# A decoder layer on one core: cross-attention scores from 12-bit halves in two halves of the array, feed-forward biases as matmul rows, Silu out of PSUM

## Chip, core and metric

One core of a Trainium2 chip runs the whole kernel in one launch. The metric is the device time in microseconds (us). A difference of about 0.3% (5.5 us) is what the measurement can tell from no change.

## What is computed

The reference is one post-norm decoder layer over 32 batches of 128 tokens, model width 512, all in float32:

```python
x = layernorm(x + attn(x, Wq, Wk, Wv, Wo))        # 16 heads of 32, rotary, causal
x = layernorm(x + xattn(x, ctx, ctx, gamma))      # 8 heads over the token axis
x = layernorm(x + ffn(x, w1, b1, ln_g, ln_b, w2, b2))

def xattn(q, k, v, gamma):     # q, k, v: [32, 128, 512], read as [batch, 8 heads, 16, 512]
    qk = einsum('bhdq,bhdl->bhql', qh, kh) / 4    # contracts 16 tokens: 512 x 512 per head
    return gamma * einsum('bhql,bhdl->bhdq', softmax(qk), vh)

def ffn(x):
    h = silu(bitlinear158(x, w1, b1))             # 512 -> 2048
    h = gelu(h)                                   # exact
    h = layer_norm(h, ln_g, ln_b)
    return bitlinear158(h, w2, b2)                # 2048 -> 512

def bitlinear158(x, w, b):     # rows of rms-normalized x to int8 steps, w to {-1, 0, 1}
    return act_quant(rms_norm(x)) @ weight_quant(w).T + b
```

## The kernel before

**Two phases.** The first phase does the self attention of all 32 batches and leaves in DRAM, for each batch, the normalized result (`x1d`), the parts of the cross attention's queries (`qd`) and keys (`kd`), and the values beside columns of ones (`cd`). The second phase does cross attention and feed-forward, batch by batch.

**The order of the work** is found by a planner (`Plan`) while the program is built. Every step is put in with `pl.op(kind, cost, fn, ins, outs, prio)`. `run` takes, again and again, the step that could start first by the given costs; ties within `slack` go by `prio` plus an offset of its kind (`OFF1`, `OFF2`). Steps of one kind keep their order. The instructions of each engine (PE, DVE, ACT, POOL, SP) are then held in the order found. Tiles come from rings: a new tile of a tag waits until the one n before it has been read. `rel` keeps a transfer from being planned before a time; in the second phase this is 30 us a batch. SP issues every DMA.

**First phase, for each batch**: `stage_q` projects queries, keys and values from float32 numbers held in two 12-bit parts (float32r), three products of parts each (`project`, L322). `stage_s` computes scores on 32 rows of the array (L419), masks them, takes the softmax, and transposes (L442). `stage_o` weighs the values (L461), applies Wo, adds x and normalizes. `split3` (L326 to L340) cuts the result and the context into three bfloat16 parts: two casts to bfloat16 (L330 on DVE, L335 on ACT), two subtractions (L333 on POOL, L336 on DVE), and six stores each (L339), because the six rows of parts of a token lie side by side in DRAM. `early` loads the operands of the first batches when the last projection has been put in. The feed-forward weights are cut to {-1, 0, 1} on the way.

**Second phase, for each batch:**

- `load` fetches operands of four heads at a time: `kp` and `qp`, 96 rows (6 rows of parts for each of 16 tokens), one DMA each (L626).
- `b1_` finds the largest score of each query: 32 matmuls of 96 rows by 512 columns (`mx`, L653), each reduced by DVE (L657). `shift` cuts its negative into three bfloat16 parts by five small operations (on POOL, L676 to L680; on DVE for the last five batches, L670 to L673), transposes them (L685, L687) and stores them as rows 96 to 98 of `qp` (L691).
- `b2_` computes the scores again, transposed, with the three rows more: 32 matmuls (`sT`, L746), each followed by an Exp out of PSUM (L749 on ACT). For each 128 keys, four heads are weighed and summed side by side, each in 32 columns of the array, in float32 (`acc`, L756). The ones beside the values give the sums of the weights.
- `final` stores the sums (L767), loads them turned (L828, L829), divides (L832, L833, L839), adds x1 and normalizes.
- `up_` scales the rows to int8 steps (`scales`, L854 to L866; `steps`, L880 and L883), adds b2 to a copy of x2 (L920), turns the steps by a DMA transpose (L922) and multiplies with w1 in four pieces of 512 columns (L933), in one bank of PSUM. DVE takes each piece out: z = piece x scale + b1 (L936).
- `gelu_` does Silu and Gelu over 2048 columns in SBUF (L948, L950). ACT loads a function table ahead of Silu, of Gelu and of the next Exp.
- `down_` takes the layer norm over 2048 columns (sums of squares on ACT, L963; one quarter normalized on ACT, L780, three on POOL, L784; ln_g and ln_b on POOL, L980; in the last five batches on DVE, L988 and L999), the mean square (L1005) and the largest value (L1006), the steps (`q2`: half on ACT, L897, half on DVE, L899, as int16, then a cast on DVE, L902), the transpose (L1011), 16 matmuls with w2 (L1017), the sum with x2 + b2 (L1021), the last norm and the store (L1024).

PSUM's banks in the second phase: three `mx`, three `sT`, one `acc`, one `m` for both feed-forward products.

Of the kernel before, what the change touches and what calls it, by code (L numbers as in the profile page):

```python
# [11 lines left out]
F32 = mybir.dt.float32  # L12
# [12 lines left out]
NB = 32  # batches  # L25
S = 128  # tokens of a batch
D = 512  # model width
NH = 16  # heads of the self attention
HD = D // NH
XH = 8  # heads of the cross attention, over the token axis  # L30
XD = S // XH
DI = 2048  # width of the feed-forward part
# [3 lines left out]
MAGIC = 12582912.0  # 1.5 * 2**23: adding it rounds to the nearest even integer  # L36
NEG = -1e30

# A float32 number is the sum of three bfloat16 parts a, b, c.  The scores of the cross attention
# contract 16 tokens only, so the products of the parts lie side by side on the contraction axis:  # L40
# six rows of parts for each token, and three rows that take the parts of the shift away.
Q_PARTS = (0, 1, 2, 0, 1, 0)
K_PARTS = (0, 0, 0, 1, 1, 2)
NPR = 6 * XD
NROW = NPR + 3

# columns of the constants
# [4 lines left out]
def constants():  # L52
    """Rotary tables by position."""
# [10 lines left out]
CFG = dict(y0e='Pool', x2be='Pool', q2T=1, q1=2, tb2=5, boost=1.0, bank_mT='mx', bank_q1T='m', bank_z='m', bank_q2T='mx', bank_py='m', early=5, gm=1, ssv=1, NQ=4, cT=3, f=2, num=1, x1=2, rden=2, x2=2, nb=32, mx=3, sT=3, acc=1, m=1, ex=8, mTe='DVE', acce='ACT', q1e='ACT', q2e='ACT', mse='Pool', lne='Pool', ye='Pool', sce='Pool', mxw=1, stw=1, pair=1, z=3, xb=3, slack=0.126, last_mse='DVE', last_lne='DVE', last_ye='Pool', last_sce='DVE', last_y0e='Pool', last_bank_mT='sT', last_bank_q1T='m', last_bank_z='m', last_bank_q2T='mx', last_bank_py='sT', zm='APPP', last_zm='F', q1m='mp', q2m='ad', last_q1m='mp', last_q2m='d')  # L64
OFF2 = {'Pool.zt': 32.97, 'Pool.zb': 10.12, 'SP.q1T': -33.89, 'SP.q2T': -25.03, 'SP.const': 8.3, 'x.kq': 7.58, 'SP.v': 6.3, 'PE.mx': 32.55, 'DVE.mx': 46.29, 'Pool.ms': -11.15, 'PE.mT': -51.04, 'DVE.mT': -18.04, 'SP.m': -65.66, 'PE.sT': -34.55, 'ACT.ex': -64.48, 'PE.pv': 35.35, 'ACT.acc': -108.33, 'SP.f': 28.74, 'SP.fd': 34.31, 'SP.fn': -21.32, 'SP.fx': -30.95, 'DVE.rd': -5.27, 'SP.fr': -64.53, 'SP.fb': -9.3, 'Pool.y': -5.46, 'DVE.y': -83.63, 'DVE.c1': 49.52, 'Pool.c1': -87.98, 'Pool.x2b': 9.33, 'PE.c1': 38.82, 'DVE.z': -130.28, 'ACT.gelu': 43.8, 'DVE.nmu': -9.46, 'ACT.sq': 102.74, 'Pool.zn': 16.77, 'ACT.sq2': 71.51, 'DVE.am2': 94.88, 'Pool.c2': -54.15, 'DVE.q2': -34.78, 'PE.c2': 62.57, 'DVE.c3': 95.97, 'Pool.c3': -68.79, 'SP.out': -62.35, 'SP.kq': 54.02, 'DVE.zn': 19.87, 'DVE.q2a': -3.2, 'DVE.ms': 82.72, 'DVE.zb': 34.45, 'ACT.q2a': 7.79, 'Pool.q1a': -75.82, 'DVE.q1': 41.56, 'Pool.yn': 0.05, 'Pool.c1m': 7.06, 'ACT.zt': -9.94, 'Pool.c2m': -14.95, 'Pool.c3n': 10.85, 'DVE.yn': 22.22, 'DVE.c1m': 4.44, 'DVE.c2m': -7.16, 'DVE.c3n': 10.04}
# [3 lines left out]
class Buf:  # L69
    """A tile that its first write allocates; n tiles of its tag rotate."""  # L70

    def __init__(self, tag, make):
        self.tag, self.make, self.t = tag, make, None
        self.left, self.free_at = 0, 0.0
        self.readers, self.writers = [], []


class Op:
    __slots__ = ("kind", "engine", "cost", "fn", "deps", "bufs", "new", "at", "rel", "prio", "end", "lat")


class Plan:
# [57 lines left out]
    def start(self, o):  # L140
# [5 lines left out]
        for b in o.new:  # L146
            n, hist = self.tags[b.tag][:2]
            if len(hist) >= n:
                if hist[-n].left:
                    return None  # L150
# [942 lines left out]
```

## Time and profile before

| | us |
|---|---|
| three executions | 1843.21, 1847.17, 1843.22 |
| median | 1843.22 |
| span of the profiled execution, first to last instruction | 1837.6 |
| median less span | 5.6 |
| busy: PE, DVE, ACT, POOL | 1694.8, 1630.8, 1337.6, 1256.5 |

The span is that of one profiled execution; the profile holds no other time of it. The first phase's last matmul starts near 681 us, the second phase's first near 683 us.

How to read its rows. A group row has the line of the kernel, the engine, the operation, the tiles (out<-in), their shapes and the count; after the bar the busy time of the group, the mean in ns of one instruction, then the engine's idle time just ahead of them and what ended it. A row of the chain of waits has a start, a length and what the end hung on in that time. In the slices each digit is the busy tenth of a fortieth of the span. PE's busy time is modelled from pipelined matmuls: a full row doesn't mean peak speed.

### The profile page before, as it was taken

What the parts mean: (1) busy time and instruction counts of PE and PEld (TensorE: products, weight loads), DVE (VectorE), ACT (ScalarE), POOL (GpSimd) and SP (SyncE); (2) the same over time, 40 slices, a digit from 0 to 9 for tenths busy, and PEclk for the clock granted to TensorE, in tenths of its full rate; (3) what the DMA queues carried; (4) which work ended last, traced back from release to release, by engine and by line L of the source; (5) the groups of instructions that cost most, each with busy time, mean ns of one, the idle gap of its engine ahead of it and who ended that gap; (6) DMA issues with size and microseconds to landing.
All of it is one profiled execution on the core that took longest, in us unless ns stands there. A gap on an engine that the chain in (4) does not pass through costs nothing.

```text
span 1837.6 us, 29788 instructions
## 1 busy us (share of the span) xinstructions
PE 1694.8 (92%) x9540; PEld 848.8 (46%) x9540; DVE 1630.8 (89%) x2811; ACT 1337.6 (73%) x2811; POOL 1256.5 (68%) x1903
## 2 busy tenths in 40 slices
PE   6999999999999989999999999999999998889864
PEld 5877777777777762232323333333333322222221
DVE  7789998889988868898989999999999989999885
ACT  3556545664545544789999989999999979878862
POOL 4466666656656550467798989899889986775562
PEclk9999999999999987998999999999999999989976
DMA  6466656665654564543545455454544543533422
GB/s 197 136 212 210 193 191 205 210 212 187 203 175 161 174 212 171 149 116 106 148 122 159 110 134 147 126 149 117 151 137 128 154 118 110 147 106 102 97 61 57
DMA packets 237733, 275.75 MB, mean 150 GB/s; under 512 B 112124, under 2 KB 161276, under 8 KB 237192
## 3 DMA queue, kind: packets, MB, share of 16 engines
q1 hardware_dynamic: 237576, 273.85, 50.2%
q8 instruction: 75, 1.23, 0.3%
q14 instruction: 82, 0.67, 0.1%
HBM read 150.82 MB, written 101.20 MB: 137 GB/s over the span
## 4 chain that ended last, share of the span: by engine, by line
PE 47%; DVE 23%; DMA 9%; ACT 7%; POOL 6%; issue 4%; SPq 1%; DVEq 0%; POOLq 0%; ACTq 0%
PE mm L322 14%; DVE mt L657 7%; PE sT L746 7%; PE acc L756 7%; PE mx L653 6%; PE sc L419 5%; ACT ex L749 3%; PE m L933 3%; PE m L1017 2%; DMA qd<-sp 2%; PE tr L442 2%; DMA q2T<-q 1%; DVE z L936 1%; DVE pr L422 1%; DMA qp<-qd 1%
## 5 line engine op out<-in xcount | busy, mean ns | idle before, releaser
L657 DVE TENSOR_REDUCE mt<-mx 128x1 f32<-128x512 f32 x1024 | 642.4, 678 | 42.7 <-PE mx L653 41.5
L749 ACT ACTIVATE ex<-sT 128x512 f32<-128x512 f32 x1024 | 535.6, 618 | 90.7 <-PE sT L746 71.8
L653 PE MATMUL mx<-kp,qp 96*128 96x512 bf16 x1024 | 342.3, 393 | 34.4 <-DVE mt L657 28.4
L746 PE MATMUL sT<-qp,kp 99*128 99x512 bf16 x1024 | 322.9, 388 | 10.8 <-ACT ex L749 6.3
L756 PE MATMUL acc<-ex,cT 128*32 128x512 f32 x2048 | 275.7, 613 | 0.7 <-DMA cT<-cd 0.7
L430 ACT ACTIVATE pr<-pr,nm 128x128 f32<-128x128 f32 x512 | 199.5, 392 | 103.9 <-DVE nm L425 87.2
L653 PEld LDWEIGHTS <-qp 96*128 96x128 bf16 x1024 | 96.5, 99 | 221.9 <-issue 120.9
L746 PEld LDWEIGHTS <-kp 99*128 99x128 bf16 x1024 | 88.3, 98 | 222.5 <-issue 146.5
L445 ACT COPY prT<-tr 128x512 f32<-128x512 f32 x96 | 52.9, 587 | 149.2 <-PE tr L442 149.0
L419 PE MATMUL sc<-qkT,qkT 32*128 32x128 f32 x1024 | 147.8, 283 | 11.6 <-DVE pr L422 11.1
L933 PE MATMUL m<-w1q,q1T 128*128 128x512 fp8e4 x512 | 137.4, 392 | 22.0 <-DVE z L936 12.4
L419 PEld LDWEIGHTS sc<-qkT,qkT 32*128 32x128 f32 x1024 | 123.4, 186 | 52.2 <-DVE pr L422 22.1
L980 POOL TENSOR_TENSOR z<-z,g_b 128x512 f32<-128x512 f32 x108 | 139.5, 1302 | 4.9 <-ACT z L780 4.3
L980 POOL TENSOR_TENSOR z<-z,bb_b 128x512 f32<-128x512 f32 x108 | 139.8, 1301 | 1.4
L435 POOL TENSOR_TENSOR pr<-pr,rd 128x512 f32<-128x512 f32 x96 | 106.4, 1108 | 45.9 <-DVE rd L433 31.8
L386 POOL TENSOR_TENSOR ra<-ra,rb 128x256 f32<-128x256 f32 x64 | 47.3, 738 | 117.4 <-DVE rb L381 117.1
L1017 PE MATMUL m<-w2q,q2T 128*128 128x512 fp8e4 x432 | 112.3, 388 | 3.8 <-DMA q2T<-q 2.8
L422 DVE TENSOR_TENSOR pr<-sc,cmask 128x512 f32<-128x512 f32 x128 | 86.8, 678 | 18.3 <-PE sc L419 10.1
L1017 PEld LDWEIGHTS <-q2T 128*128 128x128 f16 x512 | 52.3, 104 | 105.0 <-DMA q2T<-q 29.1
L936 DVE SCALAR_TENSOR_TENSOR z<-m,dq,b_b 128x512 f32<-128x512 f32 x128 | 94.9, 741 | 6.0 <-PE m L933 5.4
L430 ACT ACTIVATION_READ_ACCUMULATOR pr<-pr,nm 128x1 f32 x512 | 96.5, 189 | 0.0
L756 PEld LDWEIGHTS acc<-ex,cT 128*32 128x32 f32 x2048 | 41.2, 108 | 119.5 <-issue 112.8
(159 smaller groups left out, 3475.3 us busy)
## 6 DMA issues: line engine op xcount, KB each, us to landing
kd<-sp SPq DMA_DIRECT2D x192, 128.0 KB
qd<-sp SPq DMA_DIRECT2D x192, 128.0 KB
kp<-kd SPq DMA_DIRECT2D x64, 384.0 KB
qp<-qd SPq DMA_DIRECT2D x64, 384.0 KB
cd<-v SPq DMA_DIRECT2D x32, 512.0 KB
cT<-cd SPq DMA_DIRECT2D x32, 512.0 KB
F<-f SPq DMA_DIRECT2D x64, 256.0 KB
xt<-in_xT SPq DMA_DIRECT2D x32, 256.0 KB
```

The source lines that it names most:

```text
L322: nc.tensor.matmul(pq.t, parts[a].t[:, c, :], w[t][:, c, sl], start=k == 0, stop=k == 11)
L419: nc.tensor.matmul(sc.t[:, c * P:(c + 1) * P], qT.t[r, c, :], kT.t[r, c, :], start=True, stop=True)
L430: nc.scalar.activation(pr.t[:, c, :], pr.t[:, c, :], AF.Exp, bias=nm.t[:, c:c + 1], accum_out=den.t[:, c:c + 1])
L653: nc.tensor.matmul(sc.t[:, j, :], q.t[0:NPR, h, (qc + j) * P:(qc + j + 1) * P], k.t[0:NPR, h, :], start=True, stop=True)
L657: pl.op("DVE.mx", 0.064 + 0.534 * W, lambda: nc.vector.tensor_reduce(mt.t[:, i:i + W], sc.t, AX.X, ALU.max), (sc,), (mt,), p, join=True)
L746: nc.tensor.matmul(sc.t[:, i, :], k.t[:, h, lc * P:(lc + 1) * P], q.t[:, h, :], start=True, stop=True)
L749: pl.op("ACT.ex", 0.052 + 0.426 * SW, lambda: nc.scalar.activation(ex.t[:, j:j + SW, :], sc.t, AF.Exp, scale=1.0 / XD ** 0.5), (sc,), (ex, ...
L756: nc.tensor.matmul(acc.t[32 * h:32 * h + 32, :], v.t[:, XH * lc + 4 * g + h, :], exs[h // 2].t[:, h % 2, :], start=lc == 0, stop=lc == NC - 1)
L933: nc.tensor.matmul(flat(pz)[:, i * 512:(i + 1) * 512], q1T.t[:, c, :], w1q[:, c, (n + i) * 512:(n + i + 1) * 512], start=c == 0, stop=c == ...
L936: pl.op("DVE.z", 0.13 + 0.535 * W, lambda: nc.vector.scalar_tensor_tensor(z.t[:, sl], flat(pz), dq1.t, b1_b[:, sl], ALU.mult, ALU.add), (p ...
L980: pl.op(e + kind, 0.148 + 0.0021 * w if e == "Pool" else 0.05 + 0.00105 * w, lambda: en(e).tensor_tensor(t(), t(), other[:, sl], op), src, ...
L1017: nc.tensor.matmul(flat(py)[:, 0:D], q2T.t[:, c, :], w2q[:, c, :], start=c == 0, stop=c == NI - 1)
```

## The change

1. **Two 12-bit parts for three bfloat16 parts.** `split3` becomes `split2`: a rounding to float32r (ACT) and one subtraction (POOL for the context, DVE for the queries), and two stores of twice the size in place of six. Scores are hi x hi + lo x hi + hi x lo: 48 rows for 16 tokens. The shift is one row, no longer three: `shift` has only a transpose and a negating copy on DVE; its five small operations go, and of three stores two are left.
2. **Two heads in halves of the array.** One head's 48 or 49 rows lie on partitions 0 to 48, the next one's on 64 to 112. Each matmul of `mx` and `sT` then names rows of one half, and the planner takes a matmul right behind one in the other half as costing 0.06 us. `fetch` needs four DMAs for a tile, where one did.
3. **Biases as matmul rows.** b1 and b2 are kept in two 12-bit parts as rows (`rows1`, `rows2`). For each quantization the inverse of the back scale is formed in parts on DVE, transposed on PE and copied by DVE to `uT`; a matmul of three rows adds bias / scale to the product in PSUM. The bias add on DVE (L936) and x2 + b2 on POOL (L920) go, and the copies of b1 and b2 on all partitions.
4. **Silu read from PSUM**, with the scale, four times 512 columns. From the first Silu of a batch to its Gelu the planner puts no Exp between ("window"), and counts 1.28 us for a change of table.
5. Placement: all quarters of the layer norm on POOL (`zm='PPPP'`), q2's steps on POOL with the rounding on DVE (`q2m='mp'`); any of eight PSUM banks for any use, `m=2`; more tiles of `x2`, `z`, `q1T`; the weighing of all but the first 128 keys planned in two halves of 256 columns; 29 us a batch in `rel`; new offsets.

```diff
-def split3(kind, v, dst, parts, prio): ...
+def split2(kind, v, dst, prio):
+    sp = pl.buf("sp")
+    e, e1 = C1[kind + '_hi'], C1[kind + '_lo']
     pl.op(f"{e}.{kind}", ..., lambda: cp(e)(sp.t[:, 0, :], v.t), (v,), (sp,), prio)
+    pl.op(f"{e1}.{kind}l", ..., lambda: en(e1).tensor_tensor(
+        sp.t[:, 1, :], v.t, sp.t[:, 0, :].bitcast(F32), ALU.subtract), (v, sp), (sp,), prio)
+    for s in range(2):
+        dma(kind, lambda s=s: nc.sync.dma_start(dst[s].rearrange("t h c -> h t c"), sp.t[:, s, :].bitcast(F32)), 262, ...)
...
+def fetch(t, d, g, keys):
+    rows = t.bitcast(F32).rearrange("(p r) j c -> p r j c", p=2)
+    src = d[:, :, 4 * g:4 * g + 4, :].rearrange("s t (p j) c -> p (s t) j c", p=2)
+    for p in range(2):
+        if keys:
+            nc.sync.dma_start(rows[p, 0:XD], src[p, 0:XD])
+            nc.sync.dma_start(rows[p, XD:NPR], src[p])
+        else:
+            nc.sync.dma_start(rows[p, 0:2 * XD], src[p])
+            nc.sync.dma_start(rows[p, 2 * XD:NPR], src[p, 0:XD])
...
+sc, i, r = pl.buf("mx"), 8 * h + 4 * j + qc, slice(HALF * h, HALF * h + NPR)
+pl.op("PE.mx", 0.23, lambda: nc.tensor.matmul(sc.t, q.t[r, j, qc * P:(qc + 1) * P], k.t[r, j, :],
+                                             start=True, stop=True), (q, k), (sc,), p, half=h)
...
+mT, pt = pl.buf("mT"), bank(b, 'mT')
+pl.op("PE.mT", 0.12, lambda: nc.tensor.transpose(flat(pt)[0:16, 0:P], mt.t, ident), (mt,), (pt,), at)
+pl.op("DVE.mT", 0.2, lambda: nc.vector.tensor_scalar(mT.t, flat(pt)[0:16, 0:P], -1.0, None, ALU.mult), (pt,), (mT,), at)
...
+def inverse():
+    e = en(e2)
+    r = ut.t.rearrange("p (g r) -> p g r", r=32)
+    nc.vector.reciprocal(u.t, dq.t)
+    e.tensor_scalar(r[:, :, 0:3:2].bitcast(F32R), u.t.unsqueeze(2).to_broadcast([P, 4, 2]), 1.0, None, ALU.mult)
+    e.tensor_tensor(r[:, :, 1], u.t.to_broadcast([P, 4]), r[:, :, 0], ALU.subtract)
+pl.op(f"PE.{p}u", 0.12, lambda: nc.tensor.transpose(pt.t[:, 0:P], ut.t, ident), (ut,), (pt,), prio)
+pl.op(f"DVE.{p}u", 0.2, lambda: nc.vector.tensor_copy(uT.t, pt.t[:, 0:P]), (pt,), (uT,), prio)
...
-    pl.op("DVE.z", ..., lambda: nc.vector.scalar_tensor_tensor(z.t[:, sl], flat(pz), dq1.t, b1_b[:, sl], ALU.mult, ALU.add), ...)
+    def mm(cs, last=False):
+        for c in cs:
+            nc.tensor.matmul(pz.t, q1T.t[:, c, :], w1q[:, c, sl], start=c == 0, stop=False)
+        if last:
+            nc.tensor.matmul(pz.t, uT.t[32 * n:32 * n + 3, :], rows1[32 * n:32 * n + 3, :], start=False, stop=True)
+    pl.op("ACT.silu", 0.478, lambda: nc.scalar.activation(z.t[:, sl], pz.t, AF.Silu, scale=dq1.t),
+          (pz, dq1), (z,), at, join=True, tab="silu", win=win)
```

## The prediction

> **What bounds the kernel now.** I read the page's slices first, to find the stages.
>
> ```profile
> PE   6999999999999989999999999999999998889864
> DVE  7789998889988868898989999999999989999885
> ACT  3556545664545544789999989999999979878862
> POOL 4466666656656550467798989899889986775562
> ```
>
> Each digit is 46 us. Up to about 660 us (self attention) only PE is full. From 790 to 1440 all four engines are nearly full; then comes a thinning tail. The windows view by stage says how nearly (its columns: stretch and length, busy us of PE, PE loads, DVE, ACT, POOL):
>
> ```profile
> 184.00:552.00 368.00, 357.93 (x2398) 284.95 (x2396) 327.02 (x613) 198.60 (x739) 236.85 (x278) 0.99 0.60 197
> 1120.00:1443.00 323.00, 309.81 (x1610) 102.10 (x1606) 311.69 (x509) 304.69 (x459) 289.77 (x490) 0.99 0.50 137
> 1443.00:1700.00 257.00, 232.65 (x1163) 71.81 (x1156) 238.36 (x404) 217.15 (x329) 190.01 (x295) 0.95 0.45 120
> ```
>
> The second row holds ten batches (Gelu to Gelu), 32.3 us each: DVE 31.2, PE 31.0, ACT 30.5, POOL 29.0 us per batch. No engine has two microseconds to spare, so relief of one of them is worth at most the distance to the next. The costliest groups there:
>
> ```profile
> L657 DVE TENSOR_REDUCE mt<-mx 128x1 f32<-128x512 f32 x317 | 198.8, 677 | 6.0 <-PE mx L653 5.8
> L936 DVE SCALAR_TENSOR_TENSOR z<-m,dq,b_b 128x512 f32<-128x512 f32 x40 | 29.7, 742 | 2.0 <-PE m L933 1.6
> ```
>
> Last, the chain of waits between the phases:
>
> ```profile
> 663.57 7.87 DMA qd<-sp
> ...
> 677.42 5.37 DMA qd<-sp
> 682.81 5.41 DMA qd<-sp
> 688.24 5.41 DMA qd<-sp
> 693.67 5.41 DMA qd<-sp
> ...
> 711.01 0.99 PE acc L756 x8
> 712.00 0.75 PE sT L746 x3
> ...
> 721.35 0.65 PE mx L653 x3
> ```
>
> For 36 us the end hangs on stores of query parts, six DMAs a batch at 0.574 us of SP each. The last three lines price a change of PE's tiling: three full-array matmuls take 0.65 us after their like (0.217 each), 0.75 after the column-tiled weighing. In the records of the trace going in costs 0.09 as well: about 0.1 us per change.
>
> **Part 1: PE, cross-attention scores.** Removed: 64 bf16 matmuls a batch of 96 or 99 rows at 0.217 = 13.9 us. Added: 64 of 48 or 49 rows in 12-bit (f32r) form, alternately in the upper and lower half of the array. From the order of the changed kernel I count 800 places where two neighbours lie in different halves and 448 matmuls alone, so 25 pairs and 14 singles a batch. A single costs 0.234 (the spacing of the f32r projections, L322). No row shows a pair in row halves: at best it costs one stream, 0.22, at worst two singles, 0.47. The nearest row is the weighing, whose four column groups do run side by side (eight matmuls of 0.43 in 0.99); I take 0.26. Sum 25 x 0.26 + 14 x 0.234 = 9.8 us.
>
> Against this stands a rule of the Trainium skill ("TensorEngine Tiling (Array Packing)", Key Properties): changing the tiling mode drains TensorE. The lines above agree for column tiling, 0.1 us a time. The order has 603 runs of equal tiling in the second phase before and 1647 after: half-array scores, whole-array feed-forward, column-tiled sums and three-row bias matmuls alternate. That is 18.8 and 51.5 changes a batch, 1.9 us and 5.2 us. Without the rule PE would drop to 27.4 us; with it:
> before 13.9 + weighing 6.8 (8 x 0.85 streaming) + feed-forward 6.9 (32 x 0.217) + transposes 0.3 + changes 1.9 = 29.8;
> after 9.8 + 6.8 + 6.9 + bias rows 1.2 (5 x 0.234) + float32 transposes 0.9 (four of 0.22) + changes 5.2 = 30.8.
> What the halves win, the changes of tiling take back.
>
> **Part 2: DVE.** Removed: the bias add out of PSUM, 4 x 0.742 = 2.97 us a batch, and the half-and-half rounding of q2 (L899 1.25 + L902 0.97 = 2.2). Added: one float32-to-float16 step over 2048 columns (L883 takes 0.41 us at least for 512, so about 1.4, and there loses 0.7 waiting: 2.1). Further, twice a batch, the inverse scale: a reciprocal (0.165, L433), two tiny operations, a copy from PSUM (0.21, L687). Like operations on DVE are those of the shift in the last batches, in the groups of the page's view by line:
>
> ```profile
> L671 DVE SCALAR_TENSOR_TENSOR mr<-mt,ms 128x16 f32<-128x16 f32 x10 | 8.4, 837 | 0.3
> L670 DVE TENSOR_SCALAR ms<-mt 128x16 bf16<-128x16 f32 x10 | 5.4, 537 | 0.1
> ```
>
> Their shortest take 0.174 and 0.154. "SBUF — State Buffer" of the Trainium skill (Who interferes with whom) says that DVE operations with two SBUF inputs or in a two-port mode, and GpSimd, exclude each other for a whole instruction. With the shortest times the set costs 0.66 us; with a full GpSimd instruction (L671's median, 1.19) for both, 2.75. I take the mean wait of the four shift operations, 0.4 each: 1.33 a set, 2.7 a batch. DVE after: 31.2 - 2.97 - 2.2 + 2.1 + 2.7 = 30.8 (29.5 to 33.6).
>
> **Part 3: ACT and POOL.** ACT loses its half of q2 (1.2) and a quarter of the normalization (0.83); Silu in four pieces from PSUM costs 4 x 0.52 (the spacing of Exp, same form) against 1.91, +0.2. Table loads stay three a batch (93 in both orders). But Silu now waits for matmuls between two table loads, and no Exp may go between. Two banks hold the pieces; the third piece's five matmuls (4 x 0.217 + 0.234 + two changes 0.2 = 1.3 us) start when Silu 1 frees a bank and end 0.8 after Silu 2, and the fourth again 0.8 late: 1.6 us. Queued behind are all Exps, and PE behind three full score banks. ACT: 30.5 - 2.0 + 0.2 + 1.6 = 30.3. POOL loses the shift parts (2 x 1.24), x2 + b2 (1.27) and nb (0.19), gains a normalization quarter (0.79) and q2's 2048 columns (2.1 to 2.75, from L880's 0.685 for 512; I take 2.3): 28.1.
>
> **Part 4: SP and transfers.** Per batch 12 loads are added at 0.37 to 0.43 (16 small ones for 4) and two shift stores (0.58) go: +3.7 us, queued before shift stores and sums; some 14 us of issues become 18 of 32, so nothing to 0.3 us. In the first phase 8 of 12 stores a batch go (4.6 us of SP), and 2.2 us of DVE; but PE is 97% busy there and waited only 8.8 us for DVE between 200 and 550: -3 us (0 to -12).
>
> **Sum.** Steady, 22 batches: the busiest engine goes 31.2 to 30.8, but three engines now lie within 0.5, and PE, ACT and DVE wait for each other inside the Silu window. I let the period's excess over the busiest grow from 1.1 to 1.8: +0.3 a batch, +7. Between the phases: the chain's five last batches need 1.5 us of SP each where they took 4.3 to 4.7, but the early operand loads grow from 12 to 40 DMAs (+10 us): -12 (-20 to +5). Filling (700 to 790, PE the chain): -5. Tail, where DVE is 93% busy: shift parts of ten groups 22.4 us gone (L670 to L673), bias adds 14.9, inverse scales +13.5: -24, of which the last 50 us, a chain of q2T transposes and matmuls at half clock, hide a quarter: -18. Total 7 - 12 - 5 - 18 - 3 = -31. The profiled span of 1837.6 would become 1807; the median of the runs is 5.6 above that span, so 1812.
>
> **Rivals.**
> - *Likeliest (0.42)*: as summed, 1812, its own range 1790 to 1850.
> - *The period falls (0.20)*: pairs at 0.22 (PE 29.8), tiny DVE operations rarely blocked (29.5), Silu's waits filled. The period loses 1.3 instead of gaining 0.3: 35 better, 1777. For it speaks that bank waits already hide some changes of tiling; against it, GpSimd at 90%.
> - *Slower, PE (0.14)*: the halves do not run side by side. 64 x 0.234 = 15.0 puts PE at 36.0 and the period above 36: +4 x 22 = +88, so about 1893. It decides from a pair time of 0.27 to 0.29, where PE passes DVE. For it: no row of before has row halves at work. Against: column groups do it.
> - *Slower, DVE (0.14)*: each tiny operation waits out a GpSimd instruction: DVE 33.6, +2.8 x 22 = +62, half of the tail's gain gone: near 1870. L671's median is for it; the other three shift operations are usually short.
> - *Nothing (0.10)*: losses and gains of the ends cancel within 0.3% (5.5 us, about what can be told from no change): 1843.
>
> Chances: of the first case 0.36 lie below 1837.7 and 0.06, where the tail's gain fails, above 1848.7. Faster 0.36 + 0.20 = 0.56; the same 0.10; slower 0.14 + 0.14 + 0.06 = 0.34. The range leaves out the PE case and the best of the second: 1768 to 1875.
>
> **What would show it.** In the changed profile: the score matmuls' spacing in pairs (0.26 or 0.47) and PE's chain pieces after each change of tiling; the mean of the two inverse-scale operations on DVE against 0.15; ACT's idle before Silu waiting for PE (1.6 us a batch); Gelu-to-Gelu 32.6; the first Exp of the second phase near 690 instead of 706. I am wrong if the steady period moves by over one microsecond either way, or if the second phase starts no earlier.

## The result, and the profile after

The changed kernel takes 2080.34 us (median of four executions, 2074.62 to 2088.44) against 1843.30: 1.128 times as long (95% interval 1.125 to 1.131). The prediction was 1812 us, with a range to 1875: the sign is wrong. The profiled execution took 2074.62 us, with a span of 2072.8.

The slices of the page, as they were read before (each digit now 52 us):

```profile
PE   6999999999998899999999999999999899998975
DVE  6778887788776866877777686778777765786775
ACT  3665556564554557787766776688777665674772
POOL 3456665566553024766666774768756754653262
PEclk9999999999999877998988798898988786686786
```

One engine is full now, PE, nearly from end to end; DVE, ACT and POOL, which stood mostly at 8 or 9 beside it, stand mostly at 5 to 8. And the last row has changed, TensorE's granted clock. Before it was:

```profile
PEclk9999999999999987998999999999999999989976
```

In the windows view (stretch, length, busy us of PE, PE loads, DVE, ACT, POOL, then the granted clock, the DMA share and GB/s) for the first phase and two stretches of the second:

```profile
184.00:552.00 368.00, 365.12 (x2488) 293.74 (x2487) 301.27 (x583) 202.90 (x766) 221.25 (x269) 1.00 0.56 177
850.00:1000.00 150.00, 148.28 (x844) 53.42 (x843) 111.64 (x201) 113.17 (x181) 98.18 (x147) 0.88 0.44 112
1000.00:1250.00 250.00, 241.12 (x1284) 88.73 (x1282) 185.73 (x332) 179.28 (x281) 166.97 (x237) 0.83 0.43 109
```

Before, the same column read 0.99 in the steady second phase. PE is 96 to 99% busy at a clock that is granted for 83 to 88% only.

From Gelu to Gelu (batches 6 to 24) the period is 41.8 us, 33.1 before. Busy time in such a period, before and after: PE 31.4 and 40.0, DVE 31.3 and 30.5, ACT 30.5 and 30.1, POOL 28.8 and 27.1. Where the 235 us lie: to the first Gelu 778 us (795 before), -17; 26 periods of 41.2 (33.6), +198; from there to the end 223 us (169), +54.

The view of waits (engine, what waited, for whom: us, times, longest) says whom the others wait for:

```profile
DVE mt L710 <- PE bank L708: 252.5, 195, 8.2
ACT ex L773 <- PE bank L771: 195.0, 194, 7.6
...
ACT z L975 <- PE bank L972: 101.2, 70, 6.2
```

All three are PE. Exp's wait for its score matmul before:

```profile
ACT ex L749 <- PE sT L746: 71.8, 92, 4.3
```

The groups of the page that answer to DVE's reduction and to the score matmuls (busy us, mean ns, idle ahead of them):

```profile
L710 DVE TENSOR_REDUCE mt<-bank 128x1 f32<-128x512 f32 x1024 | 653.5, 682 | 260.9 <-PE bank L708 252.5
...
L771 PE MATMUL bank<-qp,kp 49*128 49x512 f32 x1024 | 366.0, 550 | 23.3 <-DVE mt L710 16.0
L708 PE MATMUL bank<-kp,qp 48*128 48x512 f32 x1024 | 367.9, 513 | 10.7 <-DVE mt L710 7.9
```

And DVE's reduction before:

```profile
L657 DVE TENSOR_REDUCE mt<-mx 128x1 f32<-128x512 f32 x1024 | 642.4, 678 | 42.7 <-PE mx L653 41.5
```

The reduction takes what it took (682 ns, 678 before), but DVE now idles 261 us ahead of it, where it idled 43.

### The profile page after: what moved, and what is told of

The parts are those of the page before. It is cut to its first block, busy times and chain, and to the rows that moved or that the text cites. A ratio compares the mean times of both kernels' runs of the same rounds, so it can differ in the third digit from the quotient of the medians.

```text
span 2072.8 us, 33297 instructions
## 1 busy us (share of the span) xinstructions
PE 1940.8 (94%) x11300; PEld 997.4 (48%) x11300; DVE 1543.0 (74%) x2779; ACT 1327.5 (64%) x2853; POOL 1161.7 (56%) x1599
## 5 line engine op out<-in xcount | busy, mean ns | idle before, releaser
L710 DVE TENSOR_REDUCE mt<-bank 128x1 f32<-128x512 f32 x1024 | 653.5, 682 | 260.9 <-PE bank L708 252.5
L773 ACT ACTIVATE ex<-bank 128x512 f32<-128x512 f32 x1024 | 542.8, 606 | 253.2 <-PE bank L771 195.0
L771 PE MATMUL bank<-qp,kp 49*128 49x512 f32 x1024 | 366.0, 550 | 23.3 <-DVE mt L710 16.0
L708 PE MATMUL bank<-kp,qp 48*128 48x512 f32 x1024 | 367.9, 513 | 10.7 <-DVE mt L710 7.9
L780 PE MATMUL bank<-ex,cT 128*32 128x256 f32 (+1 forms) x3584 | 346.5, 481 | 0.0
L771 PEld LDWEIGHTS bank<-qp,kp 49*128 49x128 f32 x1024 | 150.6, 212 | 251.7 <-ACT ex L773 98.0
L708 PEld LDWEIGHTS bank<-kp,qp 48*128 48x128 f32 x1024 | 166.9, 216 | 155.7 <-DVE mt L710 56.2
L1052 PE MATMUL bank<-w2q,q2T 128*128 128x512 fp8e4 x512 | 175.3, 449 | 14.5 <-DMA q2T<-q 14.4
L970 PE MATMUL bank<-w1q,q1T 128*128 128x512 fp8e4 x512 | 163.3, 436 | 2.3 <-DMA q1T<-q 2.0
L975 ACT ACTIVATE z<-bank,dq 128x512 f32<-128x512 f32 x128 | 85.9, 686 | 101.6 <-PE bank L972 101.2
```

The lines of the kernel that those rows point to most:

```text
L708: pl.op("PE.mx", 0.23, lambda: nc.tensor.matmul(sc.t, q.t[r, j, qc * P:(qc + 1) * P], k.t[r, j, :], start=True, stop=True), (q, k), (sc,), ...
L710: pl.op("DVE.mx", 0.598, lambda: nc.vector.tensor_reduce(mt.t[:, i:i + 1], sc.t, AX.X, ALU.max), (sc,), (mt,), p, join=True)
L771: pl.op("PE.sT", 0.23, lambda: nc.tensor.matmul(sc.t, k.t[r, j, lc * P:(lc + 1) * P], q.t[r, j, :], start=True, stop=True), (k, q), (sc,), ...
L773: pl.op("ACT.ex", 0.478, lambda: nc.scalar.activation(ex.t[:, h, :], sc.t, AF.Exp, scale=1.0 / XD ** 0.5), (sc,), (ex,), p, join=True, tab ...
L780: nc.tensor.matmul(acc.t[32 * h:32 * h + 32, cols], v.t[:, XH * lc + 4 * g + h, :], exs[h % 2].t[:, h // 2, cols], start=lc == 0, stop=last)
L970: nc.tensor.matmul(pz.t, q1T.t[:, c, :], w1q[:, c, sl], start=c == 0, stop=False)
```

## What PE's time consists of

Two things can be separated in the records, the work at full clock and the clock. The clock of each stretch is in the trace, so I took only stretches at full clock between the first Gelu and the 27th, summed the time from each matmul's start to the next one's (PE's idle time taken out) by kind, and scaled it to one batch. A change of tiling is then part of the kind ahead of it, so that the sums are firmer than the single columns. us for a batch at full clock:

```
                 scores  weighing  feed-fwd  bias rows  transposes   sum   share of time at half clock
prediction         9.8      6.8       6.9       1.2        0.9      30.8 (with 5.2 for changes)   -
before            15.6      8.0       7.1        -         0.3      31.1     0.04
after             15.0      8.3       8.2       2.1        0.9      34.4     0.33
bf16_halves       12.5      8.4       8.2       2.1        0.9      32.1     0.24
whole_rows        19.5      8.5       6.2       2.1        0.4      36.7     0.05
whole_bf16        16.3      8.5       7.4       2.1        0.6      35.0     0.05
rows64            15.1      8.4       8.2       2.1        0.9      34.6     0.17
no_bias_rows      15.2      8.3       8.1        -         0.8      32.4     0.38
rows64_bf16       12.7      8.4       8.2       2.1        0.8      32.2     0.13
```

(The other rows are the experiments below.) In stretches at half clock the changed kernel's sum is 60.3. With 0.33 of the time there, 1 / (0.67/34.4 + 0.33/60.3) gives 40.1 us a batch, and 40.0 was measured. So of the 9.2 us by which the prediction's 30.8 is short, 3.6 are the sum at full clock and 5.6 are the clock. Against the kernel before the sum at full clock grew by 3.3: bias rows 2.1, feed-forward 1.1, transposes 0.6 and weighing 0.3, while the scores, which were to cost 9.8 and a share of the changes, shrank by 0.6 only.

Why the clock? The stretches at half clock are whole multiples of 3.41 us. For each such slot between the first Gelu and the 27th I added up the share of the array at work: rows and columns that each matmul names, as a part of 128 x 128, times its streaming time at full clock. That is 2.4 columns of the moving operand a ns (a long row at half clock shows 512 in 0.427 us, half of this), and twice the time for each of the two records of a float32 matmul (a weighing of 256 columns takes 0.433 us). At half clock half as much fits into a slot. In the changed kernel the 21 full-clock slots that were followed by half clock had shares of 0.14 to 0.365, the 189 that were followed by full clock 0.369 to 0.77. In the kernel before, 8 slots with 0.19 to 0.38 and 237 with 0.37 to 0.93. The time in which anything streams does not separate them in the changed kernel: 0.21 to 0.71 against 0.45 to 0.85. Nor does PE's rest: in the slots before a fall PE was busy for 40 to 100% of the time, in four of the 21 for 97% or more.

The way back has the same bound. Half-clock slots of the changed kernel that stayed at half had shares of 0.02 to 0.38, those that were followed by full clock 0.35 to 0.47. In the 14 kernels of the layer here, between 700 and 1800 us, a single bound of 0.375 sorts 98 of 100 slots, both directions taken together. So half clock can hold itself, since it halves the work that fits into a slot. The median full-clock slot that stayed there has 0.76 in the kernel before, and half of this just reaches the bound; in the changed kernel it has 0.56, and half of this does not. The counts fit this: in the kernel before the clock falls 8 times and is down for 11 slots; in the changed kernel it falls 21 times and is down for 103.

This gave the theories. *Clock theory*: the clock follows the share of the array that works, and 48-row matmuls are too little, whether PE rests or not. *Load theory*: the clock is a side issue; float32r weight loads (0.183 us) lie open, and time is lost at each change of tiling. A third suspect was the bias rows.

## The experiments

Edits to the changed kernel leave the order of the instructions alone unless it is said otherwise.

**1. mixes**: long rows of matmuls of 512 columns, alone.

```
def half_f32r(h): r = slice(64 * h, 64 * h + 49); matmul(bank, q[r, ...], k[r, :])
def pair(): half_f32r(0); half_f32r(1)
200 x pair; 200 x half_f32r(0); 250 x (both halves in bfloat16); 250 x half_bf16(0);
100 x (pair, whole bf16); 25 x (4 pairs, 4 whole); 80 x (pair, weighing); 120 x weighing;
80 x (2 whole, weighing); 100 x (whole bf16, 3 rows)      # shortened; whole f32r between
```

> This kernel is not the layer: it issues only long rows of matmuls on constant operands, one mix after the other, without a wait between them, and writes zeros. Two theories of the 9 us that PE takes longer for a batch. Clock theory: the granted clock follows how much of the array works (rows x columns x streaming time, in stretches of 3.41 us), not whether PE has something to do. Then 200 matmuls in one half alone (49 rows, about 0.25 to 0.38 of the array) fall to half clock and stay there, in float32r and in bfloat16, with PE 100% busy; pairs of bfloat16 halves (0.77) stay at full clock; pairs of float32r halves (about 0.50) and pair-then-whole (about 0.45) lie at the edge. Load theory: the clock does not depend on the mix, all stretches stay at 1.0 after the start; a float32r pair takes 0.33 us because its weight loads of 0.183 us lie open, a bfloat16 pair 0.22, and a lone pair between whole-array matmuls 0.5 to 0.6 us with the drain, so that pair-then-whole takes 0.75 to 0.85. The two may both hold: the spacing at full clock tests the second, the granted clock the first.

The windows view, PE's columns and the clock: pairs in float32r; one half in float32r; one half in bfloat16; pair-then-whole; whole array and three rows in turn.

```profile
100.00:140.00 40.00, 40.00 (x356) 33.08 (x354) 0.00 (x0) 0.00 (x0) 1.00 0.01 1
175.00:245.00 70.00, 70.00 (x166) 53.66 (x165) 0.00 (x0) 0.00 (x0) 0.50 0.00 0
...
350.00:400.00 50.00, 50.00 (x233) 21.81 (x232) 0.00 (x0) 0.00 (x0) 1.00 0.00 1
430.00:500.00 70.00, 70.00 (x281) 26.16 (x279) 0.00 (x0) 0.00 (x0) 1.00 0.00 0
900.00:1005.00 105.00, 105.00 (x167) 32.32 (x167) 0.00 (x0) 0.00 (x0) 0.50 0.00 0
```

PE is 100% busy in each row, and in two of them the clock is 0.50 throughout. So the clock is not bound to PE having something to do. The expectation held for float32r; one half in bfloat16, expected to fall, stayed. The spacings at full clock: a float32r pair 0.226 us (not 0.33: in a long row its loads are hidden), a bfloat16 pair 0.215, pair-then-whole 0.756 for three, four pairs and four whole 2.09, a weighing of 256 columns 0.433 alone, 0.994 with a pair and 1.104 with two whole ones, whole and three rows 0.746 for two. The way into the halves and back thus costs 0.31 to 0.34, whole to column tiling and back 0.24, and a bias row 0.53 with all that it brings.

**2. row_counts**: where the bound lies, and whether values matter.

```
250 x one half: float32r with 64 and 56 rows; bfloat16 with 44, 40, 33 rows; zeros in bfloat16 with 44 and 64 rows
150 x pair whose two results are read by DVE and ACT, in float32r and in bfloat16
```

> Not the layer: long rows of matmuls again, with whole-array float32r between them, and zeros written. In the first such run 49 rows in float32r alone (0.355 of the array by rows and spacing) fell to half clock, 49 rows in bfloat16 (0.383) did not. If the clock follows the share of rows named, with a bound between these: 64 and 56 rows in float32r (0.46, 0.41) stay at 1.0; 44, 40 and 33 rows in bfloat16 (0.34, 0.31, 0.26) fall; with zeros for operands 44 rows fall and 64 stay, as with other values. If it follows the values, both rows of zeros fall; if float32r itself is what counts, bfloat16 stays at 1.0 down to 33 rows. Last, pairs of halves whose results are read (4 columns, one half by DVE, one by ACT): if waiting for a bank is what holds back the weight load inside a float32r matmul, float32r pairs go from 0.226 to about 0.33 us and bfloat16 pairs stay near 0.22; if not, both stay.

64 and 56 rows in float32r, 44 rows in bfloat16, 44 and 64 rows of zeros:

```profile
30.00:90.00 60.00, 60.00 (x267) 44.96 (x266) 0.00 (x0) 0.00 (x0) 0.00 (x0) 1.00 0.00 1
120.00:175.00 55.00, 55.00 (x244) 44.63 (x243) 0.00 (x0) 0.00 (x0) 0.00 (x0) 1.00 0.00 1
205.00:300.00 95.00, 95.00 (x224) 31.89 (x223) 0.00 (x0) 0.00 (x0) 0.00 (x0) 0.50 0.00 0
590.00:680.00 90.00, 90.00 (x213) 31.20 (x212) 0.00 (x0) 0.00 (x0) 0.00 (x0) 0.50 0.00 0
715.00:765.00 50.00, 50.00 (x234) 21.73 (x233) 0.00 (x0) 0.00 (x0) 0.00 (x0) 1.00 0.00 0
```

40 and 33 rows fell too. Zeros do as other values do: the rows that an instruction names count. With the spacings, 0.355 of the array (49 rows, one in 0.233 us) falls to half clock and 0.383 (49 rows in 0.216) does not, which is where the layer's own slots part. The second half of the expectation failed: with readers a float32r pair takes 0.279 us and a bfloat16 pair 0.268, so a bank that is waited for is not shown to hold back a weight load.

**3. rows64**: the clock theory in the layer.

```diff
-slice(HALF * h, HALF * h + NPR)      # mx; NROW for sT
+slice(HALF * h, HALF * h + HALF)     # 64 rows, both
```

> The changed kernel with one edit: each half's score matmuls name 64 rows where they named 48 or 49; the 15 rows more are zeros in both operands, and the stale shift that the first pass then reads only moves the softmax's shift (16 clears of operand tiles at the start of the second phase are added, some 5 us at most). Instructions, order, streams, loads and waits stay; only the share of the array that a score matmul names rises from 0.38 to 0.50. Clock theory by named rows: the stretches at half clock shrink by a half or more, mean clock of the second phase from 0.83 to 0.90 or above, time 1960 to 2050. Load theory, or a clock that follows the values that toggle (zeros add none): unchanged, 2070 to 2095.

1963 us (1949 to 1969), 1.062 of before (1.057 to 1.068): 117 us less by naming 15 or 16 more rows that hold zeros (in the first pass one of them holds an old shift).

```profile
850.00:1000.00 150.00, 148.19 (x884) 53.60 (x882) 113.64 (x206) 115.95 (x185) 106.34 (x153) 0.92 0.47 119
1000.00:1250.00 250.00, 241.11 (x1394) 90.08 (x1397) 196.37 (x351) 194.91 (x304) 172.18 (x247) 0.93 0.45 114
```

PE is as busy as in the changed kernel, 148 of 150 and 241 of 250 us, but at 0.92 and 0.93 for 0.88 and 0.83, and it gets 1394 matmuls done in the second stretch for 1284. The sum at full clock is unchanged (34.6), the share at half clock halved: the clock falls as often (19 times, 21 in the changed kernel), but it is down for 51 slots, not 103. The clock theory holds.

**4. whole_rows, bf16_halves, whole_bf16**: halves or whole array, float32r or bfloat16.

```diff
-r = slice(HALF * h, HALF * h + NPR)          # whole_rows, whole_bf16
+r = slice(0, HALF + NPR)
-matmul(sc.t, q.t[r, j, ...], k.t[r, j, :])   # bf16_halves, whole_bf16
+matmul(sc.t, q.t[r, j, ...].bitcast(BF16)[:, 1::2], k.t[r, j, :].bitcast(BF16)[:, 1::2])
```

> The changed kernel with one edit: each score matmul names rows 0 to 111 (112 with the shift) where it named 48 or 49 rows of one half, so that it multiplies two heads at once and the scores are the sums of two heads (this part of the computation is changed; loads, order and all other instructions stay, but for 16 clears of operand tiles at the start of the second phase, some 5 us at most). No two matmuls run side by side any more: 64 streams of 0.234 us a batch, 15.0 us, where pairs should have saved half. Clock theory: 0.88 of the rows work, the clock goes back to 0.95 or more in the second phase; PE 34 to 35 us a batch, period about 35.5 instead of 41.8, time about 1915 (1870 to 1950). Load theory alone, with the clock left at 0.86: PE's changes between half and whole arrays go (some 20 a batch, 4 us), the doubled streams cost 5 us, no gain: 2050 to 2110. If the halves do what the prediction took them for (0.26 a pair), the edit adds 5 us a batch: 2200.

1972 us (1967 to 1974), 1.070 (1.066 to 1.075). The clock came back to 0.97, as expected, but the time missed its range by 22: scores take 19.5 us at full clock, not 15.0.

> The changed kernel with one edit: the score matmuls read the upper 16 bits of the same float32r operands as bfloat16 (every second element; scores lose precision, this part is changed). Halves, order, rows, transfers stay; weights are loaded by instructions of their own (0.095 us in the kernel before) instead of 0.183 inside the matmul. Load theory: pairs take 0.22 to 0.26 as the prediction had it, the drains stay, PE 31 to 33 us a batch at full clock; with the clock at 1.0 the time would be 1830 to 1860. Clock theory on top of it: the array's share in a batch is about 0.58 on average (scores 64 x 0.216 x 0.38 = 5.3, weighing 6.8, feed-forward 6.9 of 33 us), so stretches below 0.48 still occur and the clock stays near 0.9: period 36 to 38, time 1920 to 1980. If neither weight loads nor the clock matter, nothing changes: 2080.

1940 us (1933 to 1957), 1.055 (1.048 to 1.061), inside what load and clock theory together gave (the period, 38.8, just above it). Scores fell from 15.0 to 12.5, and the clock stayed low (0.24 of the time at half).

> The changed kernel with both edits of the two runs before it together: the score matmuls name rows 0 to 111 (112) and read the upper 16 bits as bfloat16 (scores are sums of two heads at lower precision: this part is changed). It is the fourth corner of halves or whole rows by float32r or bfloat16. PE's sum for a batch, by the spacings measured so far: scores 64 x 0.216 = 13.8, weighing 6.9, feed-forward 6.9, bias rows 5 x 0.53 = 2.65, float32 transposes 1.5, changes to and from the weighing 11 x 0.24 = 2.7: 34.5. If clock, open weight loads and the bias rows explain the period of 41.8 between them, the clock is above 0.96 and the period 35 to 36, the time 1880 (1850 to 1910). If the two edits each took away the same thing, it stays with them at 38.8 and 1940 to 1970.

1920 us (1918 to 1926), 1.041 (1.037 to 1.044), 10 above its range; PE's sum is 35.0 (34.5 expected), the period 37.5, because PE idles 2.1 us of it. Read as a square, PE's sums are 34.4 and 36.7 us in float32r and 32.1 and 35.0 in bfloat16 (halves, whole). The scores' column alone differs more, 15.0 and 19.5, 12.5 and 16.3, but part of what it gains stands in its neighbours' columns (feed-forward 8.2 and 6.2). So the halves do save, 2.3 to 2.9 us of the sum; float32r gives 1.7 to 2.3 back; and the 15.0 for scores comes out near the 15.6 of the kernel before. The load theory holds as a size, not as the whole cause.

**5. no_bias_rows**:

```diff
-    nc.tensor.matmul(pz.t, uT.t[32 * n:32 * n + 3, :], rows1[32 * n:32 * n + 3, :], start=False, stop=True)
-    nc.tensor.matmul(py.t, uT.t[0:3, :], rows2, start=False, stop=True)
```

> The changed kernel without the five matmuls a batch of three rows that add b1 and b2 (the biases are left out; the inverse scales, their transposes and copies stay). In the trace each takes 0.09 us of drain and 0.42 us to the next matmul, 0.51 at full clock where the prediction had 0.234 and a share of the changes. Load theory: 2.6 us a batch less at full clock, about 3 at the clock of 0.86: period 38.8, time about 2005 (1985 to 2025). Clock theory: beside that, a stretch with three rows at work lowers the array's share, and without it fewer stretches fall to half clock: 1960 to 2005. If the bias rows hide beside other waits: above 2060.

2017 us (2004 to 2034), 1.097 (1.088 to 1.106): inside the load theory's range. The sum at full clock lost its 2.1 us, but the share at half clock rose from 0.33 to 0.38, against what the expectation made of the clock theory, so that the period fell by 1.2 only. Why it rose is not shown.

**6. weigh512**: the weighing in one step again.

```diff
-for i in range(m): pl.op("PE.pv", ..., lambda cols=...: weigh(cols, last), ...)
+for i in range(m): pl.op("PE.pv", ..., lambda i=i: weigh(slice(0, D), last) if i == 0 else None, ...)
```

> The changed kernel with the weighing of each 128 keys in one step of 512 columns, at the place of the first of its two steps; the second is empty, all else stands in the same order. Runs of half-array matmuls go from 650 to 550, changes of tiling from 1667 to 1439, 7 a batch. At 0.31 us for a round trip and 0.3 for fewer short steps 1.4 us a batch at full clock: period about 40, time 2030 (2000 to 2060). If the second step's place hid in waits of PE: 2075 to 2090. If the weighing in one piece makes Exp wait longer for banks: slower.

2027 us (2019 to 2034 in three executions, 2070 in a fourth), 1.101 (1.097 to 1.105), the time that was expected, but not by the way expected: the sum at full clock is 34.2 (34.4), the steady period 41.4 (41.8), and 24 us of the gain lie behind the 27th Gelu. So seven changes of tiling fewer did not show in the sum; the price of a change is that of the long rows in 1, and in the layer's order it is not confirmed one by one.

**7. rows64_bf16 and rows64_bf16_no_bias**: the edits added up.

> The changed kernel with two of the edits together: 64 rows named in each half, and the upper 16 bits read as bfloat16 (scores of lower precision: this part is changed). By the spacings at full clock of the bfloat16 halves PE needs 32.1 us a batch; naming 64 rows halved the share of half clock (0.33 to 0.17 in float32r), so 0.24 should become about 0.10: PE 33.5, period 35.8, time 1860 (1835 to 1890). If the clock were bound to something else than the rows named, as in the run with 49 rows: 1940.

1897 us (1887 to 1911), 1.033 (1.029 to 1.037): 7 above the range. PE 34.0 us a batch (33.5 expected), the clock 0.13 at half (0.10), but PE idles 3.0 us.

> As the run before it, and without the bias rows (b1 and b2 are left out too). PE at full clock 29.9, at 0.10 of half clock 31.3, so DVE (30.5), ACT (30.1) and PE lie together as the prediction had them: period 33, time 1790 (1765 to 1825), below the kernel before. If it stays above 1843, PE is not the only thing that makes the changed kernel slower, and the sums of DVE, ACT and POOL or their waits are to be looked at.

1874 us (1872 to 1877), 1.018 (1.016 to 1.020). This expectation failed. One of its windows:

```profile
1000.00:1250.00 250.00, 221.53 (x1401) 59.09 (x1401) 202.93 (x360) 196.21 (x314) 185.40 (x266) 0.90 0.46 118
```

PE is down to 222 of 250 us, and no engine is full. PE needs 32.3 us of a period of 36.5 and idles 4.2: the engines now wait for one another. The order was planned for other durations (the second half at 0.06 us, any clock at full), which is a likely reason, not a tested one; by how much a new order would mend it stays open.

**8. pairs_joined and scores3**, both planned anew: a pair as one step, and the scores of the kernel before in the changed kernel.

```diff
-pl.op("PE.mx", 0.23, <one half>, (q, k), (sc,), p, half=h)   # twice     (pairs_joined; sT likewise)
+pl.op("PE.mx", 0.34, <both halves>, (q, k), scs, p)
-split2, fetch, shift of the changed kernel                              (scores3)
+split3, one DMA a tile, shift in three parts of the kernel before
```

> The changed kernel with each pair of half-array matmuls put in as one step of the planner (0.34 us, two banks at once), so that no half stands alone; the order is planned anew. In the order the runs of half-array matmuls go from 650 to 556 and none has an odd length (199 of 650 had one matmul, 97 three); all changes of tiling from 1667 to 1478. Load theory: 224 streams that ran alone (0.23) and 94 round trips of tiling (0.31) go, 2.5 us a batch at full clock; period 38.5 to 39.5, time 1990 (1950 to 2040). Clock theory: the pairs fill the array better, but time goes faster than work, the clock stays at 0.83 to 0.88. If steps of two banks make DVE and ACT wait more than PE gains: 2080 or more.

2205 us (2193 to 2209), 1.193 (1.188 to 1.198).

> Parts 3 to 5 of the change alone: the changed kernel with the scores of the kernel before (three bfloat16 parts, 96 and 99 rows, whole array, three rows of shift with its small operations, six stores, one DMA for a tile), planned anew with the changed kernel's offsets. 39 changes of tiling a batch, where the kernel before has 19 and the changed one 52: bias rows (10), weighing in two halves (6), float32 transposes. PE at full clock: 13.9 + 6.9 + 6.9 + bias rows 2.65 + transposes 1.5 + changes 3.3 = 35.2 against 31.4 before. If this is right, bias rows and split weighing cost 2 to 3 us a batch although DVE is relieved: 1885 (1850 to 1920). If the whole loss comes from the halves, parts 3 to 5 gain what the prediction gave them: 1800 to 1843.

2102 us (2092 to 2113), 1.137 (1.130 to 1.144). Both far above what was expected, with periods that swing from 11 to 100 us. So the next run asked what a new order costs by itself.

**9. replanned**:

```diff
-CFG = dict(..., slack=0.1, ...)
+CFG = dict(..., slack=0.126, ...)
```

> The changed kernel with one number of the planner changed: ties within 0.126 us are decided by priority, where 0.1 stood. No instruction is added or taken away, only their order differs. It measures what planning anew with offsets found for another plan costs, which the two replanned runs (pairs as one step, 2205; scores of the kernel before, 2102) contain beside their edit. If a mere new order is nearly free: 2060 to 2100, and then the joined pairs themselves cost 125 us. If the order is what made them slow: 2130 or more, and nothing can be read from those two runs on their edits.

2200 us (2184 to 2208), 1.192 (1.186 to 1.199): a different order alone costs 119 us, with half clock for 0.46 of the steady time. Nothing can be read from the two times of 8 on their edits. PE's sums at full clock say more, since a change of order alone moves them less (35.2 in this run, 34.4 in the changed kernel): 33.8 with joined pairs, the scores at 13.6 (15.5 in this run), so that halves that stand alone do cost; and 35.2 with the scores of the kernel before, which is what was expected of it. So parts 3 to 5 make PE's sum as large with the old scores as it is with the new ones. What they do to the time, in an order found for them, stays open.

**10. before_35rows**: the suspect put into the kernel before.

```diff
-matmul(sc.t[:, j, :], q.t[0:NPR, h, ...], k.t[0:NPR, h, :])         # mx; all 99 rows for sT
+matmul(sc.t[:, j, :], q.t[64:NROW, h, ...], k.t[64:NROW, h, :])     # 35 rows, both
```

> The kernel before with one edit: its score matmuls, in both passes, name rows 64 to 98 (35 rows: two of the six products of parts and the shift) where they named 96 and 99; four products of parts are left out, and four tiles of queries are cleared at the start of the second phase (some 2 us). Order, streams, types, transfers and waits stay; no pair runs side by side, since all lie in the same half. It puts the suspect into the kernel that has nothing else of the change. Clock theory: a batch's share of the array sinks from 0.86 to about 0.53 (scores 64 x 0.216 x 0.27 = 3.8, weighing 6.9, feed-forward 6.9 of 33 us), less than the changed kernel's 0.58, so a quarter to a third of the second phase falls to half clock; PE at full clock 31 to 32.5 with the changes to the half, at 0.3 of half clock 37 to 40; time 1990 to 2100. If rows matter only by pairs or by float32r: 1845 to 1870.

Four executions took 2002.3, 2057.1, 2057.1 and 2058.8 us. The profile is of the first:

```profile
720.00:800.00 80.00, 79.97 (x240) 18.00 (x240) 41.22 (x69) 34.09 (x62) 13.43 (x35) 0.50 0.37 115
850.00:1250.00 400.00, 391.04 (x1768) 102.89 (x1767) 336.27 (x559) 338.68 (x509) 306.48 (x522) 0.88 0.45 118
```

No pairs, no float32r, no bias rows; the same order, the same streams, a sum at full clock of 31.9 (31.1 before). In the kernel before, the first of these two windows reads:

```profile
720.00:800.00 80.00, 77.97 (x416) 23.75 (x409) 70.44 (x127) 59.34 (x108) 25.97 (x62) 1.00 0.55 166
```

Few rows alone cost 160 us in the profiled execution and 215 to 217 in the other three, inside the clock theory's range. Between the first Gelu and the 27th the clock fell 10 times (8 before) and was down for 74 slots (11). It is also seen that the clock is an edge: batches 4 to 16 ran at a period of 33.0 with a clock of 0.99 and lost nothing (32.7 before), batches 16 to 26 at 41.1 with 0.81 (35.3 and 0.97 before).

## Why the prediction was wrong

- **The failed step is PE's sum in part 1.** "I take 0.26" for a pair and "about 0.1 us per change" of tiling gave 30.8; at full clock it is 34.4. Halves do run side by side: neighbours start 3 ns apart, and long rows give 0.226 a pair, better than I took. But in the layer's order a pair is seldom in a long row: 650 runs of halves, 199 of them of one matmul. The way in and out costs 0.31 in long mixes, not 0.2, and within a run the next pair starts 0.332 after the last (0.235 in bfloat16). Why these loads lie open there and not in the long rows is not settled. Scores came to 15.0 with their changes; bias rows 2.1 where I had 1.2 and a share of the changes. One sign stood in the prediction itself: the same way of summing gave 29.8 for the kernel before, whose window shows 31.0 (31.1 at full clock in the table), and these 1.2 us were not carried over. With them PE would have come to 32.0, above DVE. (The order as run has 1667 runs of equal tiling, not 1647, which makes 0.06 us.)
- **A step is missing altogether: full clock was taken for granted.** Every duration was read from rows at a clock of 0.99. The change halves the rows of all 64 score matmuls of a batch, and the share of the array comes so near to the bound that a short wait of PE takes the clock down and half clock then keeps itself. That is 5.6 of the 9.2 us. Naming 64 rows (rows64) and few rows in the kernel before (before_35rows) show it from both sides. The page "TensorE: Matmul & The Clock Gate" of the Trainium skill (Part 1) says that activity releases the throttle and that an idle window of about 3.4 us brings it back. The slots of 3.41 us agree; but here half clock came with PE 100% busy in long rows, and in the layer after slots in which it was busy for 40 to 100%, and the runs decide: what counts is the array's share, not PE's rest. By the page's wording the change costs no clock, by the runs a seventh of the period.
- **The drain of the tiling page was the right objection**, and I let it weigh too little. A change of tiling does cost time here, 0.24 to 0.34 us for a round trip in long rows; with 0.31 instead of 0.2, and without the hope that pairs come in rows, PE would have been the bound in the forecast.
- **DVE held.** 30.8 predicted, 30.5 measured. The inverse scale: 0.15, 0.43 and 0.45 us for its three operations on average and 0.29 for the copy, 1.32 a set. I had 1.33, but that is luck in part: by its own terms (0.70 at the shortest, not 0.66, and twice a wait of 0.4) the set would have been 1.5, and DVE 31.1.

```profile
L905 DVE TENSOR_SCALAR ut<-u x64: 172/174/1926, 754.9 to 2056.0; 128x8 fp32r<-128x8 f32 x64
L906 DVE TENSOR_TENSOR ut<-u,ut x64: 166/168/1936, 755.5 to 2056.2; 128x4 f32<-128x4 f32 x64
```

The three numbers after the colon are shortest, median and longest: mostly free, now and then a wait of up to 1.8 us, as the row of the shift operations had shown. All 43 that took 0.3 us or more end 12 to 33 ns after a GpSimd instruction, which agrees with the exclusion that the prediction reckoned with.

- **POOL held within 1 us, ACT by chance.** POOL: 28.1 predicted, 27.1 measured. ACT: 30.3 predicted and 30.1 measured, but the 30.3 held 1.6 of waiting, so the busy time was put at 28.7. A piece of Silu takes 0.687 us, not 0.52, which is a part of the gap; and ACT waits 3.5 us a batch for its matmuls (111.8 us in all), not 1.6, which is PE again.
- **Excess of the period over the busiest engine:** 1.8 us, the predicted number, by chance: it was argued for three engines close together, and one alone was full.
- **The start held in the sum, by luck in its parts.** The first Exp of the second phase comes 15.5 us earlier (690.7, 706.2 before), as forecast; the first Gelu 17, I had 20 by then. But the first phase was to give 3 us and the way between the phases 12 (its own terms, some 15 us of stores less 10 of early loads, make 5). Measured, the first phase's last matmul starts 12.7 us earlier (669.4, 682.1 before): PE is at 99% there (97% before), idle for 2.9 us between 184 and 552 where it idled 10.1. From there to the first Exp only 2.9 us were won, and 1.4 on the way to the first Gelu, where 5 were expected.
- **The tail did not.** -18 was predicted for DVE's relief; it is +54, with the clock at 0.6 to 0.8 in the last slices. PE was the bound there too, busy for 98.9 us of the 100 from 1900 on; only the last 73 us leave it idle for more than half.
- **The rivals.** "Slower, PE" had the right engine and sign and the wrong reason (no halves side by side); its 36.0 us of PE are near the 34.4 that the changed kernel has at full clock. It was given 0.14.

## What to carry to other kernels

Before halving the rows of matmuls, work out the share of the array that will be at work in 3.4 us, rows times columns times streaming time, with what the changes of tiling take: under about 0.36 to 0.38 TensorE's clock went to half here, busy or not. Then halve it: if the half lies under the bound too, one slot of waiting can leave the kernel at half clock for many slots. A saved stream is worth its time only in long rows of equal tiling; count runs in the order, not matmuls. And test a way of summing on the kernel before, and carry over what it misses there.

## What the runs showed of the hardware

- Naming 15 or 16 more rows that hold zeros saved 117 us. In long rows of matmuls 44 rows in bfloat16 went to half clock, with zeros too; 49 rows in bfloat16, and 64 rows of zeros, did not.
- Going back to full clock has the same bound as staying there, about 0.375 of the array, if work is counted at the full-clock rate. At half clock a slot can hold half of it at most, so a mix that keeps full clock at 0.56 can stay at half clock with 0.30 (medians of the changed kernel). This may be why executions of one kernel came to 2002 and 2057 us; it was not tried.
- A matmul of three rows between whole-array ones costs 0.53 us, more than two full ones of 0.216.
- With 64 float32r matmuls of the whole array a batch, PE's sum in the layer's order is 1.7 us larger than with bfloat16 ones (36.7, 35.0), though in a long row one takes 0.228 and 0.216.
